# First layer's tanh of images 1 to 7 as Exp, Ln, Exp in chunks, with the limit on VectorE right behind the sum

## Chip, cores and metric

One core of a Trainium2 chip runs the whole program. The metric is the device time of one execution in microseconds; the median of three runs is given, and one further execution was profiled.

## The reference

Eight images of 128 channels and 36 x 36 pixels go through two layers. The change lies in the first:

```python
# layer 0, per image; xn is the group-normed image through a 1x1 convolution
q = conv3x3(xn, w_qx)                     # 36 x 36 queries
k, v = conv3x3(xn, w_kx, 'VALID'), conv3x3(xn, w_vx, 'VALID')   # 34 x 34
a_x = v @ softmax(q @ k)                  # attention over the 1156 keys
h = tanh(conv1x1([xn, a_x, context], w_h) + b_h)
x = x + conv1x1(h, w_o) + b_o
# layer 1, per image: additive attention of 1296 tokens,
#   scores = w . tanh(q_i + k_j), softmax, weighted sum; then a gated mixture of experts
```

The context term is the same for every pixel, so with b_h it is one column, `hb`. The output of layer 0 of an image is the input of its layer 1.

## The kernel before

**The main loop.** The scores of layer 1 take nearly all the time. They are written as sums of quotients of exponentials: for each image (8), chunk of 432 queries (3) and tile of 128 keys (11, the last of 16 keys), twelve *slots* (two for the last tile) each compute a denominator and a numerator by matmuls. There are 2,928 slots. In one slot, `denominators` lets TensorE make `d` in PSUM (two buffers) and ScalarE (ACT) take its Ln (L999); at the end of a group of one or two slots ACT takes Exp of minus that (L1002), the reciprocal. `numerators` lets TensorE make `n` in PSUM (four banks, shared with all other matmul results outside the scores). `terms` lets VectorE (DVE) multiply `n` by the reciprocal, either into `rp` (L1033, three buffers) that GpSimd (POOL) adds up (L1040, L1042), or in place (L1027), added up on DVE (L1029). Denominators are issued three slots ahead. At the end of a tile POOL folds the sums (L1049, L1051) and ACT takes their Exp (L1062).

**Background work.** While image b is in its main loop, image b+1 is prepared in a lane of generators: `normal`, `conv_keys`, `layer0`, `tokens`, `keys`. Each engine runs its instructions in the order in which they were issued, so the place of a background instruction in the slots sets what stands behind it. A generator says at each yield whether it goes on to matmuls (`matmuls(rest)`) or not (`step(rest)`, `TAKE` is a step without rest), and how many slots it rests first. `take_turns` runs due steps at the start of a slot (not in the four slots of twelve whose products DVE adds up itself), `matmul_turn` runs due matmuls in every third slot, after that slot's terms, as far as a pace in matmul columns allows; several turns can follow one another there.

**The first layer.** `layer0(b)` computes v, then per chunk of 432 pixels (`NCH` = 3): the queries by `conv_turns`, four turns of three matmuls `pc`, each followed at `TAKE` by copies or sums on DVE (L312 to L316); the scores `s`, their Exp on ACT (L471), the sums on POOL (L462); the weighted values `pa`, their scaling by a reciprocal made of Ln and Exp (L485, L486, L499, L500); and the convolution of x, `px`, that is added into the chunk's columns of `hp` (L506). The tile `hp` is named hpre in the profile. After the three chunks one ACT instruction takes tanh of all 1,296 columns with the bias `hb` (L509). The tanh isn't in the set of tables that has Ln and Exp, so a table load stands ahead of it (counted to L509), and `preload_act_table_set(LNEXP)` loads the other set again (L510). Then the three matmuls `po` (w_o) follow, and DVE adds them to the image (L517).

Image 0 is prepared before the main loop, with no slots around it. Images 1 to 7 are prepared in the background of images 0 to 6.

Of the kernel before, what the change touches and what calls it, by code (L numbers as in the profile page):

```python
# [11 lines left out]
AF = mybir.ActivationFunctionType  # L12
ALU = mybir.AluOpType
AX = mybir.AxisListType

NB, C, H, W = 8, 128, 36, 36
# [6 lines left out]
RC = H // NCH  # L23
# [49 lines left out]
def kernel(  # L73
# [28 lines left out]
    nc = tc.nc  # L102
# [27 lines left out]
    with ExitStack() as loop, ExitStack() as score:  # L130
# [22 lines left out]
        def big_tile(name):  # L153
            return big.tile([128, NT * 128], F32, tag="big", name=name)

        def chunk_tile(name):
            return chunks.tile([128, CH], F32, tag="chunk", name=name)

        def aux(name):
            return ps_n.tile([128, 512], F32, tag="n", name=name)  # L160
# [40 lines left out]
        ones = const.tile([128, 128], F32, tag="ones", name="ones")  # L201
# [32 lines left out]
        hb = const.tile([C, 1], F32, tag="hb", name="hb")  # L234
# [20 lines left out]
        LNEXP = "natural_log_exp_and_others"  # L255
# [16 lines left out]
        TAKE = (False, 0)  # L272

        def step(rest=1):
            return (False, rest)

        def matmuls(rest=0):
            return (True, rest)
# [3 lines left out]
        def bmm(out, lhsT, rhs, **kw):  # L282
            behind[0] += max(out.free_size(), 128) + 20
            mm(out, lhsT, rhs, **kw)  # L284
# [9 lines left out]
        def conv_turns(taps, rows, y0, dst, inner):  # L294

            r0, nr = rows
            even, odd = ((1, slice(1, WV, 2)), (0, slice(0, WV, 2))) if inner else (
                (0, slice(0, W, 2)), (0, slice(1, W, 2)))
            for j in range(4):
                ps = aux("pc")[:, : nr * HW]  # L300
                for dy in range(3):
                    bmm(ps, taps[:, dy, j, :],
                        xwin[:, j, (y0 + dy + r0) * HW : (y0 + dy + r0 + nr) * HW],
                        start=(dy == 0), stop=(dy == 2))
                yield TAKE
                ps = ps.rearrange("p (a b) -> p a b", b=HW)
                for (t0, cols), used in ((even, j < 3), (odd, j > 0)):
                    if used:
                        d = dst[:, :, cols]
                        m = ps[:, :, t0 : t0 + d.shape[-1]]  # L310
                        if j == 0 or (j == 1 and cols is odd[1]):
                            nc.vector.tensor_copy(d, m)  # L312
                        elif j == 2 and cols is odd[1]:
                            nc.vector.tensor_sub(d, d, m)
                        else:
                            nc.vector.tensor_add(d, m, d)  # L316
                yield matmuls()
# [13 lines left out]
        def load_taps(name):  # L331
            if name in raw_taps:
                return raw_taps.pop(name)[0]
            t = big_tile(name)[:, : 12 * C]
            nc.sync.dma_start(t, turned_taps[name])
            return t.rearrange("p (y j c) -> p y j c", y=3, j=4)
# [68 lines left out]
        def grid(t, width):  # L405
            return t.rearrange("p (a b) -> p a b", b=width)

        def conv_keys(b):
# [3 lines left out]
            for r0, nr in KROWS:  # L412
                yield from conv_turns(
                    taps["k"], (r0, nr), 1, grid(k[:, r0 * WV : (r0 + nr) * WV], WV), True
                )

        def layer0(b):

            r = xs[b][:, :N]
            k = convolved.pop("k")  # L420
            while gates:
                yield step()
            wv_t = load_taps("wv_t")
            v = big_tile("v0")
            wq_t = load_taps("wq_t")
            yield matmuls(3)
            for r0, nr in KROWS:
                yield from conv_turns(
                    wv_t, (r0, nr), 1, grid(v[:, r0 * WV : (r0 + nr) * WV], WV), True
                )  # L430
            yield matmuls(1)

            vw = big_tile("vw")[:DT, : NDT * C].rearrange("p (j c) -> p j c", c=C)
            for g in range(0, NDT, 4):
                some = DTILES[g : g + 4]
                tp = aux("pvw")
                for j, (o, n) in enumerate(some):
                    bmm(tp[:n, j * C : (j + 1) * C], v[:, o : o + n], wh_s[:, 1, :],
                       start=True, stop=True)
                yield TAKE  # L440
                full = sum(n == DT for _, n in some)
                nc.vector.tensor_copy(
                    vw[:, g : g + full, :],
                    tp[:DT, : full * C].rearrange("p (j c) -> p j c", c=C),
                )
                for j in range(full, len(some)):
                    n = some[j][1]
                    nc.vector.tensor_copy(vw[:n, g + j, :], tp[:n, j * C : (j + 1) * C])
                yield matmuls()
            hp = big_tile("hpre")[:, :N]  # L450
            for c in range(NCH):
                cols = slice(c * CH, (c + 1) * CH)
                q = chunk_tile("q0")
                yield from conv_turns(wq_t, (c * RC, RC), 0, grid(q, W), False)
                yield matmuls(1)
                tot = chunk_tile("tot0")
                ex = []

                def total(j):
                    n = DTILES[j][1]  # L460
                    of = ex[0] if j == 1 else tot
                    nc.gpsimd.tensor_add(tot[:n], of[:n], ex[j][:n])  # L462

                ax = chunk_tile("ax0")
                for j0 in range(0, NDT + 2, 2):
                    for o, n in DTILES[j0 : j0 + 2]:
                        ps = aux("s0")
                        bmm(ps[:n, :CH], k[:, o : o + n], q, start=True, stop=True)
                        yield TAKE
                        e = chunk_tile("e0")  # L470
                        nc.scalar.activation(e[:n], ps[:n, :CH], AF.Exp)  # L471
                        ex.append(e)
                        if len(ex) > 2:
                            total(len(ex) - 2)
                        yield matmuls()
                    if j0 == 0:
                        continue
                    if j0 == NDT:
                        total(NDT - 1)
                        yield matmuls(3)  # L480
                        ri = chunk_tile("ri0")
                        pt = aux("pt0")
                        bmm(pt[:, :CH], ones[:DT], tot[:DT], start=True, stop=True)
                        yield TAKE
                        nc.scalar.activation(ri, pt[:, :CH], AF.Ln)  # L485
                        nc.scalar.activation(ri, ri, AF.Exp, scale=-1.0)  # L486
                        yield matmuls()

                    pa = aux("pa0")[:, :CH]
                    for j in (j0 - 2, j0 - 1):  # L490
                        n = DTILES[j][1]
                        bmm(pa, vw[:n, j, :], ex[j][:n], start=(j == j0 - 2), stop=(j == j0 - 1))
                    yield TAKE
                    if j0 == 2:
                        nc.vector.tensor_copy(ax, pa)
                    elif j0 < NDT:
                        nc.vector.tensor_add(ax, pa, ax)
                    else:
                        nc.vector.tensor_add(pa, pa, ax)  # L499
                        nc.vector.tensor_mul(ax, pa, ri)  # L500
                    yield matmuls()
                px = aux("px1")
                bmm(px[:, :CH].rearrange("p (a b) -> p a b", b=W), wh_s[:, 0, :],
                   xpad[:, 1 + c * RC : 1 + (c + 1) * RC, 1 : 1 + W], start=True, stop=True)
                yield TAKE
                nc.vector.tensor_add(hp[:, cols], px[:, :CH], ax)  # L506
                yield matmuls()
            yield step(2)
            nc.scalar.activation(hp, hp, AF.Tanh, bias=hb)  # L509
            nc.scalar.preload_act_table_set(LNEXP)  # L510
            yield matmuls(2)
            for c in range(NCH):
                cols = slice(c * CH, (c + 1) * CH)
                po = aux("po0")
                bmm(po[:, :CH], wo_s, hp[:, cols], start=True, stop=True)
                yield TAKE
                nc.vector.scalar_tensor_tensor(  # L517
                    r[:, cols], po[:, :CH], bo_s, r[:, cols], ALU.add, ALU.add
                )
                yield matmuls()  # L520
# [629 lines left out]
        for p, (u, k) in enumerate(slots):  # L1150
            b, c, j = units[u]
# [181 lines left out]
    for h in range(NB // 2):  # L1333
        for c in range(NCH):
            cols = slice(c * CH, (c + 1) * CH)
# [76 lines left out]
```

## Time and profile before

| | |
|---|---|
| median of 3 runs | 6119.27 us (6111.72 to 6121.77) |
| the profiled execution | 6131.19 us |
| its span | 6129.5 us |
| mean granted TensorE clock | 0.982 |
| busy: PE, DVE, ACT, POOL | 92%, 78%, 87%, 75% |
| main loop, ACT alone: Ln L999, Exp L1002 | 2483.2 and 2495.8 us |
| tanh L509 | 8 x 1.376 us |
| table loads at L509 and L510 | 8 x 1.283 us each |

PE is TensorE's matmuls. Line numbers are of the kernel before. A row of a group gives the instructions of a line with output and inputs, shapes and count, their busy time and the mean duration in ns, and then the idle time of the engine ahead of them with what ended it. A row of a timeline gives start and duration in us, engine, line, operation and count, and in brackets the idle time of the engine ahead of it and who ended it; a matmul in fp32 stands there as two records. In a row of windows, the engines' busy times are in the order PE, weight loads, DVE, ACT, POOL; after them come the granted clock of TensorE as a share of full speed (PEclk), the busy share of the DMA engines and their GB/s.

### The profile page before, as it was taken

Reading aid. Unit: us, or ns where it says so; the run is one execution under the profiler, and the core shown is the slowest. Engines: PE = TensorE matmul, PEld = TensorE weight load, DVE = VectorE, ACT = ScalarE, POOL = GpSimd, SP = SyncE. Lnnn points to the kernel's source line nnn. Section 1 sums busy time; section 2 is a strip of 40 time slices with the busy share of each in tenths; the row PEclk is TensorE's granted clock in tenths of the full one; section 3 lists DMA queues with packets and bytes.
Section 4 is the critical chain, followed back from the end, with each engine's and each line's share of the span. In section 5 each row is a group of like instructions: output and inputs, shape, how many; then the busy total and the mean of one; then the engine's idle time right before and its main releaser. Section 6 shows DMA issues by size and latency. Waiting matters only on the chain.

```text
span 6129.5 us, 94280 instructions
## 1 busy us (share of the span) xinstructions
PE 5669.4 (92%) x33500; PEld 2928.9 (48%) x33500; DVE 4786.5 (78%) x9544; ACT 5338.2 (87%) x5859; POOL 4603.0 (75%) x2824
## 2 busy tenths in 40 slices
PE   7999999999999999999999999999999999988886
PEld 5554455544554445544445444454445544544433
DVE  4787878878788788877787777887778878788883
ACT  1999898998989989889998999899998998999991
POOL 4777777877778867778687786877777777777871
PEclk9999999999999999999999999999999999999998
DMA  1210021001110011100111001110011000110008
GB/s 44 73 34 22 25 74 40 20 25 33 66 39 20 26 46 54 37 24 23 61 39 39 22 24 65 40 33 23 28 62 49 24 25 28 66 50 29 28 20 286
DMA packets 150409, 270.42 MB, mean 44 GB/s; under 512 B 45553, under 2 KB 75633, under 8 KB 149937
## 3 DMA queue, kind: packets, MB, share of 16 engines
q1 hardware_dynamic: 149936, 264.39, 13.0%
q8 instruction: 264, 4.33, 0.3%
q14 instruction: 209, 1.70, 0.1%
HBM read 200.15 MB, written 63.93 MB: 43 GB/s over the span
## 4 chain that ended last, share of the span: by engine, by line
PE 54%; DVE 16%; ACT 15%; issue 11%; POOL 2%; DMA 1%; SPq 0%; DVEq 0%; POOLq 0%; ACTq 0%
PE d L976 18%; PE n L976 12%; ACT lq L999 11%; PE pa L284 7%; DVE rp L1033 7%; PE pc L284 5%; DVE n L1027 5%; PE s L284 3%; DVE accd L1029 2%; PE pq L284 2%; PE pk L284 1%; PE d L981 1%; PE n L981 1%; ACT e L1062 1%; DMA w<-in_weight_dram 1%
## 5 line engine op out<-in xcount | busy, mean ns | idle before, releaser
L1042 POOL TENSOR_TENSOR accp<-accp,rp 128x864 f32<-128x864 f32 x1439 | 2912.2, 2024 | 995.3 <-DVE rp L1033 951.4
L976 PE MATMUL d<-qf,kf 32*128 32x432 f32 (+1 forms) x11520 | 2785.5, 562 | 269.3 <-ACT lq L999 264.0
L976 PE MATMUL n<-qf,kf 32*128 32x432 f32 (+1 forms) x11520 | 2997.9, 556 | 31.0 <-DVE rp L1033 12.4
L999 ACT ACTIVATE lq<-d 128x864 f32<-128x864 f32 x2928 | 2483.2, 877 | 473.9 <-PE n L976 284.6
L1033 DVE TENSOR_TENSOR rp<-n,lq 128x432 f32<-128x432 f32 x3912 | 2180.2, 600 | 757.5 <-PE n L976 606.3
L1002 ACT ACTIVATE lq<-lq 128x864 f32<-128x864 f32 (+1 forms) x1944 | 2495.8, 1284 | 61.7
L976 PEld LDWEIGHTS d<-qf,kf 32*128 32x128 f32 (+1 forms) x11520 | 1024.4, 185 | 1447.4 <-ACT lq L999 1105.5
L976 PEld LDWEIGHTS n<-qf,kf 32*128 32x128 f32 (+1 forms) x11520 | 1263.1, 186 | 700.4 <-issue 294.8
L1029 DVE TENSOR_TENSOR accd<-n,accd 128x432 f32<-128x432 f32 x1440 | 866.1, 601 | 24.6
L1027 DVE TENSOR_TENSOR n<-n,lq 128x432 f32<-128x432 f32 x1440 | 810.3, 607 | 59.1 <-PE n L976 37.1
L1040 POOL TENSOR_TENSOR accp<-rp 128x864 f32<-128x864 f32 x240 | 485.6, 2023 | 286.6 <-DVE rp L1033 284.4
L284 PE MATMUL pa<-xh,e 128*108 128x129 f32 x1920 | 254.9, 281 | 32.7 <-DVE accd L1029 27.7
L284 PEld LDWEIGHTS pa<-xh,e 128*108 128x108 f32 x1920 | 221.0, 174 | 127.4 <-DVE accd L1029 102.6
L1051 POOL TENSOR_TENSOR accd<-accp,accd 128x432 f32<-128x432 f32 x239 | 265.4, 1110 | 18.7
L1049 POOL TENSOR_TENSOR accp<-accp 128x432 f32<-128x432 f32 x239 | 263.9, 1104 | 11.8
L711 POOL TENSOR_SCALAR qf<-qf,cs_s 128x432 f32<-128x432 f32 x192 | 260.3, 1366 | 9.2 <-ACT qf L710 9.2
L462 POOL TENSOR_TENSOR tot<-tot,e 116x432 f32<-116x432 f32 x192 | 212.2, 1105 | 9.0 <-ACT e L471 4.5
L284 PE MATMUL s<-q,k 128*116 128x432 f32 x480 | 207.0, 547 | 7.8 <-DVE accd L1029 5.5
L471 ACT ACTIVATE e<-s 116x432 f32<-116x432 f32 x240 | 116.3, 521 | 99.1 <-PE s L284 97.9
L284 PE MATMUL pa<-e,vw 116*128 116x432 f32 x480 | 196.8, 532 | 0.4
L284 PEld LDWEIGHTS pk<-xT,a_k 128*128 128x128 f32 x1408 | 164.8, 192 | 54.2 <-DVE accd L1029 43.5
L1022 DVE TENSOR_TENSOR accd<-n,lq 128x432 f32<-128x432 f32 x240 | 143.8, 599 | 49.6 <-ACT lq L1002 26.3
(223 smaller groups left out, 3826.5 us busy)
## 6 DMA issues: line engine op xcount, KB each, us to landing
kf<-kd SPq DMA_DIRECT2D x239, 512.0 KB
kd<-ks SPq DMA_DIRECT2D x158, 256.0 KB
w<-in_weight_dram SPq DMA_DIRECT2D x32, 1024.0 KB
wk_t<-wk_t_d SPq DMA_DIRECT2D x7, 768.0 KB
wv_t<-wv_t_d SPq DMA_DIRECT2D x7, 768.0 KB
wq_t<-wq_t_d SPq DMA_DIRECT2D x7, 768.0 KB
x<-in_x_dram SPq DMA_DIRECT2D x8, 648.0 KB
t<-tokd SPq DMA_DIRECT2D x96, 54.0 KB
```

The lines of the kernel that those rows point to most:

```text
L284: mm(out, lhsT, rhs, **kw)
L711: nc.gpsimd.tensor_scalar(qf[:, 1, :], qf[:, 0, :], cs_s[:, q : q + 1], None, ALU.mult)
L976: mm(outs[h][:, :CH], kf[rows[h], q, :], qf_of[b, c, q][rows[h], part, :], start=True, stop=True)
L999: nc.scalar.activation(lq[:, o : o + n, :], d[:, :n, :CH], AF.Ln)
L1002: nc.scalar.activation(some, some, AF.Exp, scale=-1.0)
L1027: mult(ns[h], ns[h], lq[:, o + h, :])
L1029: nc.vector.tensor_add(live["d"], ns[h], live["d"])
L1033: mult(rp[:, h, :], n, lq[:, o + h, :])
L1040: nc.gpsimd.tensor_add(live["p"], live["r"], rp)
L1042: ending(u if k == NP - 1 else 0).tensor_add(live["p"], live["p"], rp)
L1049: ending(u).tensor_add(s[:, 0, :], s[:, 0, :], s[:, 1, :])
L1051: ending(u).tensor_add(d, s[:, 0, :], d)
```

## The change

For images 1 to 7, tanh is written as tanh(y) = 1 - 2 exp(-ln(1 + exp(2y))). Each chunk's columns are treated on their own. Right behind the sum of L506, DVE adds `hb` and limits the values to 15 at most (`limited`). Three more functions are put into a queue, `late`: `exp` and `log` on ACT, and `share`, which is another Exp on ACT and a multiplication and addition on POOL. Chunks 0 and 1 have theirs taken one at a time at the `TAKE`s of the next chunk's query convolution, ahead of that turn's DVE copies. Those of chunk 2 are taken one at a time after a `step(1)` each. Exp and Ln are in the set of tables that the scores use. Image 0 keeps its tanh with the two loads, and the `step(2)` ahead of it is gone.

```diff
+        def tanh_parts(h):
+
+            def limited():
+                nc.vector.tensor_scalar(h, h, hb, 15.0, ALU.add, ALU.min)
+
+            def exp():
+                nc.scalar.activation(h, h, AF.Exp, scale=2.0)
+
+            def log():
+                nc.scalar.activation(h, h, AF.Ln, bias=ones[:, 0:1])
+
+            def share():
+                nc.scalar.activation(h, h, AF.Exp, scale=-1.0)
+                nc.gpsimd.tensor_scalar(h, h, -2.0, 1.0, ALU.mult, ALU.add)
+
+            return limited, exp, log, share
+
         def layer0(b):
...
             hp = big_tile("hpre")[:, :N]
+            late = deque()
             for c in range(NCH):
                 cols = slice(c * CH, (c + 1) * CH)
                 q = chunk_tile("q0")
-                yield from conv_turns(wq_t, (c * RC, RC), 0, grid(q, W), False)
+                for says in conv_turns(wq_t, (c * RC, RC), 0, grid(q, W), False):
+                    yield says
+                    if late and says == TAKE:
+                        late.popleft()()
                 yield matmuls(1)
+                assert not late
                 tot = chunk_tile("tot0")
...
                 yield TAKE
                 nc.vector.tensor_add(hp[:, cols], px[:, :CH], ax)
+                if b > 0:
+                    limited, *parts = tanh_parts(hp[:, cols])
+                    limited()
+                    late.extend(parts)
                 yield matmuls()
-            yield step(2)
-            nc.scalar.activation(hp, hp, AF.Tanh, bias=hb)
-            nc.scalar.preload_act_table_set(LNEXP)
+            if b == 0:
+                nc.scalar.activation(hp, hp, AF.Tanh, bias=hb)
+                nc.scalar.preload_act_table_set(LNEXP)
+            while late:
+                yield step(1)
+                late.popleft()()
             yield matmuls(2)
```

## The prediction

> **What bounds the kernel now.** I read the page first, then the ScalarE groups by line, then the timelines of all engines around one tanh (image 6's background work makes image 7's first layer, at 5146 us), then the table of windows.
>
> ```profile
> span 6129.5 us, 94280 instructions
> PE 5669.4 (92%) x33500; PEld 2928.9 (48%) x33500; DVE 4786.5 (78%) x9544; ACT 5338.2 (87%) x5859; POOL 4603.0 (75%) x2824
> ...
> L509 ACT ACTIVATE hpre<-hpre,hb 128x1296 f32<-128x1296 f32 x8 | 11.0, 1376 | 1.2 <-DVE hpre L506 1.1
> ...
> L509 ACT ACT_TABLE_LOAD x8 | 10.3, 1283 | 0.1
> L510 ACT ACT_TABLE_LOAD x8 | 10.3, 1283 | 0.1
> ```
>
> No engine is the bound everywhere: PE is busy 92%, ACT 87%. So the stretch around the change decides. There the tanh and its two table loads keep ACT from the scores for 3.98 us (5146.79 to 5150.77):
>
> ```profile
> 5146.79 1.28 ACT L509 ACT_TABLE_LOAD   x1
> 5148.09 1.38 ACT L509 ACTIVATE hpre<-hpre,hb 128x1296 f32<-128x1296 f32 x1
> 5149.48 1.28 ACT L510 ACT_TABLE_LOAD   x1
> 5150.77 0.89 ACT L999 ACTIVATE lq<-d 128x864 f32<-128x864 f32 x1
> ...
> 5151.72 0.63 PE L976 MATMUL d<-qf,kf 32*128 32x432 f32 x2 [3.88 <-ACT lq L999]
> ...
> 5154.17 1.81 PE L976 MATMUL d<-qf,kf 64*128 64x432 f32 x4 [1.27 <-ACT lq L999]
> ...
> 5157.35 3.37 PE L284 MATMUL po<-hpre,w_o 128*128 128x432 f32 x6
> ...
> 5161.69 0.89 ACT L999 ACTIVATE lq<-d 128x864 f32<-128x864 f32 x1 [3.10 <-PE n L976]
> ```
>
> See three things. PE idles 3.88 us behind the block. Then PE is slow: the four d records take 1.81 where the same row shows 1.00 at 5145.09. And ACT then loses another 3.10 us waiting for that slow PE. The windows agree (us, busy by engine, PEclk):
>
> ```profile
> 5060.00:5120.00 60.00, 57.37 (x332) 29.14 (x329) 47.63 (x96) 55.48 (x64) 53.30 (x34) 1.00 0.07 22
> 5120.00:5180.00 60.00, 52.47 (x276) 25.66 (x276) 48.52 (x106) 53.53 (x56) 38.30 (x23) 0.94 0.11 32
> ```
>
> **What the Trainium skill says.** (1) "ScalarE: Activation LUTs", sections "What ACT_TABLE_LOAD costs" and "Table sets: the hidden batching unit": a load is 1283 ns plus a drain of about 1380 ns, and natural_log_exp_and_others holds both exp and ln. The trace agrees on 1283; a drain does not show (ACT idles 0.1 us over 8 loads). (2) "TensorE: Matmul & The Clock Gate", section "What's actually happening": PE's clock halves after an idle window of about 3.4 us, until it has been busy for one. The trace has PEclk 0.94 over the 60 us with the tanh, a loss of 3.6 us, so about 7 us at half rate. (3) "VectorE: DVE Perf Modes", section "Mode 2×_2P": an fp32 tensor_scalar from SBUF to SBUF uses both read ports. The trace fits: L325, 128x384 with one input, takes 353 ns, L326 of the same size with two takes 608. (4) "SBUF — State Buffer", section "SBUF: two separate sides": such an op shares a port pair with GpSimd under an exclusive lock, and the later one blocks for the whole instruction of the other. The trace agrees, on a tensor_scalar of 11 columns:
>
> ```profile
> L260 DVE TENSOR_SCALAR ve<-ln_mv x8: 173/1693/1701, 142.6 to 5184.7; 128x11 f32<-128x11 f32 x8
> ```
>
> It takes 173 ns once, with POOL free, and about 1693 ns in the others, which run beside a POOL add of 2.02 us and end with it.
>
> **The change part by part,** for one of seven images (1 to 7).
>
> *Removed: the block.* 3.98 us of ACT, and ACT has no idle time in the 7 us before it and only 0.18 in the 8 after: all 3.98 is on the path.
>
> *Removed: the slow clock behind it.* From the d at 5154.17 to the next d at 5160.65 PE is busy 6.48 us at half rate. At full rate elsewhere: d to n 0.83 and n to the next 0.82 (5013.92, 5014.75, 5015.57), and three 432 column matmuls 2.36 (the s of 5032.08, next d 5034.44): 4.01. That is 2.47 less, and ACT's wait of 3.10 shrinks to 0.63. So 2.47 on the path too. Together 6.45.
>
> *Added on ACT: nine pieces.* Exp in SBUF is 563 ns (L486). Ln with a bias column I take as L1062's 640. Neighbours overlap by 0.09 (L1062 starts 5140.39, the next 5140.94), so a chunk's pieces cost 0.47 + 0.55 + 0.47 = 1.49. ACT's busy time rises by 3 x 1.77 - 3.94 = 1.4 us an image. Where they land decides:
> - Chunk 2's run at three successive steps in the stretch above, where ACT has no idle: 1.49 on the path. By the step counts the po matmuls keep their turn.
> - Chunk 1's exp and log are issued with the two conv turns of 5015.57, before an Ln for which ACT idles 1.47 us: free. If that cover is gone, 1.02. Its share comes with the turn of 5021.83, into 19 us without ACT idle: 0.47.
> - Chunk 0's log and share come with the turns of 4942.71, before an Ln for which ACT idles 1.31: free, with the same cost if not. Its exp waits for the limit, next.
>
> *Added on DVE: the limit,* 432 columns, SBUF to SBUF. By L325's 353 for 384 I take 0.38. It is put right behind L506, ahead of the next score products, so it depends on POOL. In chunks 1 and 2 POOL is idle at that time (its adds ended at 5012.37 and 5138.52; the limit would start at 5012.95 and 5139.2). DVE's products are 0.38 late, the PE buffers as much: I take 0.3 and 0.2, bounds 0 and 0.38 each. Chunk 0 is different:
>
> ```profile
> 4938.35 0.60 DVE L506 TENSOR_TENSOR hpre<-px,ax 128x432 f32<-128x432 f32 x1
> 4938.94 0.38 DVE L312 COPY q<-pc 128x216 f32<-128x216 f32 x1
> 4939.99 1.12 DVE L1033 TENSOR_TENSOR rp<-n,lq 128x432 f32<-128x432 f32 x2 [0.66 <-PE n L976]
> ...
> 4938.58 2.03 POOL L1042 TENSOR_TENSOR accp<-accp,rp 128x864 f32<-128x864 f32 x1 [1.19 <-DVE rp L1033]
> ...
> 4939.88 0.89 ACT L999 ACTIVATE lq<-d 128x864 f32<-128x864 f32 x1 [1.10 <-PE n L976]
> ```
>
> The POOL add starts while L506 runs and ends at 4940.61. The limit must wait for it and ends at about 4940.95. Behind it on DVE stand the copy and the products of 4939.99 (then 4941.3, 1.3 late). ACT's exp waits for the limit until 4941.0 and takes to 4941.5, and the Ln of 4939.88 stands behind that: 1.6 late. The next d on PE (4940.82) waits for this Ln, and from there PE was the bound (ACT idles 1.31, 0.90, 1.40, 1.62 for it up to 4956). So 1.6 on the path. Without the lock it would be 0 to 0.4.
>
> *Added on POOL:* three tensor_scalars of about 1.3 us (L324's mean 1268 for 384 columns, L711's 1366 for 432). POOL idles about 1.1 us between its adds there and 6.2 us ahead of the add of 5158.73; chunk 2's comes after the add that ends at 5152.5 and must be done for the last po matmul, about two slots of 2 us later. Each waits for its exp; behind it stand the score adds, and DVE for their rp buffers. ACT runs ahead of POOL by several slots, so I cost it nothing; if po waits, up to 1 us. Image 0 keeps its tanh; its dropped step stands in a part that runs without slots, so it costs nothing. No DMA is added or moved, and SP's queue is not touched.
>
> **Sum:** 6.45 - 1.49 - 0.47 - 0.3 - 0.2 - 1.6 = 2.4 us an image, 17 us for seven. The profiled execution took 6131.2, so a like one would take 6114; from the median 6119.3 it is 6102.6. What is late next: PE in chunk 0's and 1's stretches, ACT in chunk 2's.
>
> **Rivals.**
> - *No lock on the limit* (the lock is seen here on 11 columns, not on 432): chunk 0 costs 0.3 and not 1.6. 3.7 an image: 6093. Against it stand the seven blocked rows.
> - *The clock drops behind chunk 0's limit, and the kernel gets slower.* PE would idle from 4940.56 to 4942.45, 1.9 us of a window of 3.4. Drops already follow waits of 1.1 to 1.4 us near 4690 (PEclk 0.96 there). One of 6.8 us at half rate where PE is the bound costs up to 3.4: 2.4 - 3.4 = -1.0 an image, 6126. It decides where a drop costs more than 2.4 in the mean of the images, so at 3.4 it must come in five of seven.
> - *ACT becomes the bound* and hides no piece: another 1.02 for each of chunks 0 and 1: 0.4 an image, 6117. Against it: ACT's idle rows there name PE.
> - *The loads stay*, if Exp and Ln alternated between sets: six loads of 1.28 an image and more, 5.3 us slower an image, 6156. Against it: one load at the start serves all Ln and Exp of the scores now.
>
> **How the numbers follow.** The forecast has 0.42, no lock 0.17, the clock drop 0.25, ACT the bound 0.11, loads or something unseen on the slow side 0.05. 0.2% is 12.2 us, about what a measurement of this kernel tells from no change. Of the forecast's 0.42, with its bounds of about 1 us an image (6095 to 6111), 0.29 is over 0.2% faster; all of no lock is. The drop, with 0 to 3.4 us an image and drops elsewhere that shift with the phase, gives 0.10 same and 0.15 slower; ACT the bound 0.07 same and 0.04 slower. Sum: 0.46 faster, 0.30 same, 0.24 slower. For 8 in 10 the range goes from 6087 (no lock, bounds in favour) to 6130 (the drop and some waits at po).
>
> **What would show it.** Right: one tanh and two of its loads left; no drop of PEclk behind where the tanhs were; the limit's row x21 with a mean near 0.9 us, some 0.38 and seven near 2.0; the Ln behind chunk 0's exp 1.6 late; images of about 735 us where they take 737 to 741 from tanh to tanh. Wrong: all 21 limits at 0.4 (no lock); half clock right after chunk 0's limit (the drop); PE waiting for ACT at 5016 and 4943 (ACT the bound).

## The result, and the profile after

The changed kernel takes 6111.23 us (median of 22 runs, 6104.40 to 6116.83) against 6118.79 of before (22 runs, 6111.72 to 6131.01). The ratio is 0.9986, with an interval of 0.9980 to 0.9993: about 0.14% faster, 8 us. A second measurement gave 0.9982 (0.9973 to 0.9990), 10.6 us. The forecast was 6102.6 with a range of 6087 to 6130: some 17 us were expected, and 8 to 11 came.

The page after, its span, its engines, and the rows of the lines that took the place of L509 and L510 (from the groups by line: busy us, mean ns, then the idle time ahead and who ended it):

```profile
span 6106.2 us, 94348 instructions
...
PE 5658.5 (93%) x33500; PEld 2920.2 (48%) x33500; DVE 4805.0 (79%) x9565; ACT 5340.4 (87%) x5901; POOL 4615.2 (76%) x2845
```

```profile
L426 ACT ACTIVATE hpre<-hpre,ones 128x432 f32<-128x432 f32 x21 | 13.6, 646 | 0.2
...
L423 ACT ACTIVATE hpre<-hpre 128x432 f32<-128x432 f32 x21 | 11.6, 552 | 14.1 <-DVE hpre L420 14.1
L429 ACT ACTIVATE hpre<-hpre 128x432 f32<-128x432 f32 x21 | 11.6, 552 | 0.2
...
L535 ACT ACTIVATE hpre<-hpre,hb 128x1296 f32<-128x1296 f32 x1 | 1.4, 1375 | 1.1 <-DVE hpre L528 1.1
...
L535 ACT ACT_TABLE_LOAD x1 | 1.3, 1283 | 0.0
L536 ACT ACT_TABLE_LOAD x1 | 1.3, 1283 | 0.0
```

One tanh and its two loads are left, for image 0. ACT is busy 2 us more than before, not less. L423, the first Exp, carries 14.1 us of waits for the limit, L420. That limit and the last step on POOL, seen by tile (min, median and max ns):

```profile
L420 DVE TENSOR_SCALAR hpre<-hpre,hb x21: 445/446/1854, 501.3 to 5121.4; 128x432 f32<-128x432 f32 x21
...
L430 POOL TENSOR_SCALAR hpre<-hpre x21: 549/554/564, 514.4 to 5135.2; 128x432 f32<-128x432 f32 x21
```

446 ns is the limit alone. Seven of the 21, all of chunk 0, stand beside a POOL add and take 1782 to 1854 ns. Here is one, in the timeline of all engines (start, duration in us, and in brackets the idle time ahead):

```profile
4918.39 0.59 DVE L528 TENSOR_TENSOR hpre<-px,ax 128x432 f32<-128x432 f32 x1
4918.61 2.01 POOL L1071 TENSOR_TENSOR accp<-accp,rp 128x864 f32<-128x864 f32 x1 [1.18 <-DVE rp L1062]
...
4919.02 1.85 DVE L420 TENSOR_SCALAR hpre<-hpre,hb 128x432 f32<-128x432 f32 x1
...
4920.79 0.37 DVE L312 COPY q<-pc 128x216 f32<-128x216 f32 x1
4920.90 0.56 ACT L423 ACTIVATE hpre<-hpre 128x432 f32<-128x432 f32 x1 [2.09 <-DVE hpre L420]
4921.08 1.11 DVE L1062 TENSOR_TENSOR rp<-n,lq 128x432 f32<-128x432 f32 x2
...
4921.37 0.87 ACT L1028 ACTIVATE lq<-d 128x864 f32<-128x864 f32 x1
```

The POOL add ends at 4920.62 and the limit at 4920.87. Behind it stand the products (L1062) on DVE, and behind L423 the next Ln of the scores (L1028) on ACT. In the stretch of the tanh the same view shows this now:

```profile
5126.34 0.55 ACT L423 ACTIVATE hpre<-hpre 128x432 f32<-128x432 f32 x1
...
5129.29 0.64 ACT L426 ACTIVATE hpre<-hpre,ones 128x432 f32<-128x432 f32 x1
...
5132.30 0.55 ACT L429 ACTIVATE hpre<-hpre 128x432 f32<-128x432 f32 x1
...
5133.68 0.99 PE L1005 MATMUL d<-qf,kf 64*128 64x432 f32 x4 [1.90 <-ACT lq L1028]
...
5135.33 2.44 PE L284 MATMUL po<-hpre,w_o 128*128 128x432 f32 x6
...
5138.74 0.89 ACT L1028 ACTIVATE lq<-d 128x864 f32<-128x864 f32 x1 [0.93 <-PE n L1005]
```

PE's longest wait there is 1.90 us where it was 3.88. The po matmuls take 2.44 us where they took 3.37, and ACT waits 0.93 for PE where it waited 3.10. The window that answers to the 60 us around the tanh of before:

```profile
5102.60:5162.60 60.00, 55.43 (x296) 27.06 (x296) 53.77 (x118) 55.41 (x61) 42.95 (x27) 1.00 0.12 32
```

PEclk (third from the end) is 1.00, it was 0.94. This holds for the image shown. In two of the seven images of this profile, PE's clock is halved for 3.41 us behind the same wait of 1.90; d and po are then slower (compare their rows in the view before):

```profile
2189.29 1.37 PE L1005 MATMUL d<-qf,kf 64*128 64x432 f32 x4 [1.90 <-ACT lq L1028]
...
2192.03 3.00 PE L284 MATMUL po<-hpre,w_o 128*128 128x432 f32 x6
```

**Place by place.** The slots come in the same order in all these kernels, so the starts of ACT's Ln of the scores can be compared one by one. How much later (+) or earlier (-) than in the first profile of before a stretch of slots ends, relative to its begin, is the table's number: us an image, mean over images 1 to 7. Of an image's 366 slots, chunk 0 is slots 170 to 185, chunk 1 is 195 to 222, *tanh* is 264 to 289, *tokens*, the piece behind the po matmuls, is 290 to 310, and *early* is the first 80. Nothing was edited in *tokens* and *early*.

| kernel | chunk 0 | chunk 1 | tanh | tokens | early |
|---|---|---|---|---|---|
| before again | 0.00 | -0.01 | +0.01 | +0.04 | 0.00 |
| changed | +1.10 | +0.91 | -4.69 | 0.00 | -0.58 |
| changed, again | +1.10 | +0.91 | -4.46 | +0.99 | -0.49 |
| tanh left out | 0.00 | -0.01 | -6.54 | -0.36 | -0.49 |
| idle TensorE kept busy | 0.00 | -0.01 | -2.43 | +0.09 | -1.23 |
| limit alone | +0.96 | +0.48 | -0.56 | -0.27 | -1.30 |
| pieces a turn later | +0.97 | +0.92 | -4.66 | +0.66 | -0.37 |
| limit from PSUM | +0.19 | +1.04 | -4.12 | -1.00 | -1.38 |
| limit from PSUM, pieces paired | +0.19 | +0.78 | -4.14 | -0.55 | -1.15 |
| no limit | +0.01 | +0.39 | -3.82 | -0.23 | -1.20 |

The first profile of before is one of its slowest runs (6131 us, median 6119). The columns of chunks 0 and 1 can be read as they stand, because no half clock stands there in these profiles. *Tokens* and *early*, and in part *tanh*, also hold what TensorE's clock did in the two runs compared. The row of the limit alone shows by how much in *tanh*: that kernel has the tanh and its loads, and still reads -0.56. Single executions of before lie up to 20 us apart on one chip (6116.25 to 6136.75).

### The profile page after: what moved, and what is told of

Same layout as the page of the kernel before. It is cut to its first block, busy times and chain, and to the rows that moved or that the text cites. A ratio compares the mean times of both kernels' runs of the same rounds, so it can differ in the third digit from the quotient of the medians.

```text
span 6106.2 us, 94348 instructions
## 1 busy us (share of the span) xinstructions
PE 5658.5 (93%) x33500; PEld 2920.2 (48%) x33500; DVE 4805.0 (79%) x9565; ACT 5340.4 (87%) x5901; POOL 4615.2 (76%) x2845
## 4 chain that ended last, share of the span: by engine, by line
PE 53%; DVE 17%; ACT 15%; issue 11%; POOL 2%; DMA 1%; SPq 0%; DVEq 0%; POOLq 0%; ACTq 0%
PE d L1005 17%; PE n L1005 12%; ACT lq L1028 11%; PE pa L284 7%; DVE rp L1062 7%; DVE n L1056 5%; PE pc L284 5%; PE s L284 3%; DVE accd L1058 2%; PE pq L284 2%; PE pk L284 1%; PE d L1010 1%; PE n L1010 1%; ACT e L1091 1%; DMA w<-in_weight_dram 1%
## 5 line engine op out<-in xcount | busy, mean ns | idle before, releaser
L1028 ACT ACTIVATE lq<-d 128x864 f32<-128x864 f32 x2928 | 2482.5, 877 | 434.6 <-PE n L1005 260.4
L1062 DVE TENSOR_TENSOR rp<-n,lq 128x432 f32<-128x432 f32 x3912 | 2180.1, 600 | 747.2 <-PE n L1005 601.8
L284 PE MATMUL pk<-xT,a_k 128*128 128x128 f32 (+1 forms) x1408 | 180.6, 281 | 0.2
```

What stands on the lines that cost most here:

```text
L1028: nc.scalar.activation(lq[:, o : o + n, :], d[:, :n, :CH], AF.Ln)
L1062: mult(rp[:, h, :], n, lq[:, o + h, :])
```

## The experiments

**Before again.** The same program, another execution.

> The kernel before, profiled in another execution. Theory A (the block costs the same in every run): TensorE at half clock for 6.8 us behind all seven tanhs of images 1 to 7 as in the first profile, and 737 to 741 us from one tanh to the next. Theory B (the half clock depends on where TensorE's idle 3.9 us fall in the windows of 3.41 us in which the clock is set, so the profile of before, at 6131 us the slowest of its runs, showed more of it than usual): behind some of the tanhs no half clock or 3.4 us of it, the stretch from there 1 to 2.5 us shorter in those images, and a time of 6112 to 6122 us.

6126.94 us. TensorE at half clock stands behind all seven tanhs again, 6.8 us each:

```profile
5150.15 0.63 PE L976 MATMUL d<-qf,kf 32*128 32x432 f32 x2 [3.88 <-ACT lq L999]
...
5152.60 1.81 PE L976 MATMUL d<-qf,kf 64*128 64x432 f32 x4 [1.43 <-ACT lq L999]
...
5155.78 3.45 PE L284 MATMUL po<-hpre,w_o 128*128 128x432 f32 x6
```

The same 3.88 us of waiting stands there, d (1.81) runs at half rate, and so does a part of po (3.45). From tanh to tanh it takes 737.1 to 740.8 us. Theory A holds for this run. But it is a slow one too (median of before on this chip 6120.76), so alone it doesn't rule out theory B. Two runs further down speak against B. With TensorE kept busy, the medians lie 18 us apart. And with the limit alone, the profiled execution (6126.36) lies near its median (6125.86), and half clock of 6.8 us or more stands at all seven tanhs. There, though, PE's wait is 3.42 us and the half clock begins before its end in six of them, and the place is 0.56 us shorter in the mean, so where the half clock falls may matter. An execution of before at its own median was not profiled.

**Idle TensorE kept busy.** To the kernel before:

```diff
             nc.scalar.preload_act_table_set(LNEXP)
+            if b > 0:
+                yield step(1)
+                warm = aux("warm")
+                for _ in range(5):
+                    mm(warm[:, :CH], wo_s, r[:, :CH], start=True, stop=True)
             yield matmuls(2)
```

> The kernel before with five matmuls of 432 columns put into TensorE's idle 3.9 us behind each tanh, their results unused. ACT's block of 3.98 us stays. Theory A: the half clock behind the tanh goes, 2.47 us in each of seven images, 17 us: 6102 us, like the changed kernel. Theory B: the half clock is there only in a part of the executions, so 5 to 10 us are won: about 6110 us. Rival C (the extra matmuls stand ahead of the scores' and delay them): 0.5 us an image is lost where no half clock was, and the time is 6117 to 6122 us.

6102.69 us, ratio 0.9968 (0.9955 to 0.9980): 18 us faster, with the tanh, its loads and ACT's block untouched. The stretch of the tanh ends 2.43 us earlier in the mean (2.15 to 2.65 in single images), close to the 2.47 that the prediction worked out for the slow clock. PE is busy where it idled, and the po matmuls are back at full rate (timeline of this kernel):

```profile
5124.52 3.89 PE L515 MATMUL warm<-x,w_o 128*128 128x432 f32 x10
...
5133.60 2.44 PE L284 MATMUL po<-hpre,w_o 128*128 128x432 f32 x6
```

Theory A. Five matmuls whose results nobody reads gain 18 us, more than the 8 to 11 of the change.

**Without the tanh.** The tanh of images 1 to 7, its bias and its loads are left out of the kernel before.

> The kernel before without the tanh of images 1 to 7 and without its two table loads (that part of the computation is left out; the bias goes with it). It shows what removing the block is worth before anything is paid for. Theory A: 3.98 us of ACT and 2.47 us of slow TensorE an image, 45 us: 6074 us. Theory B: 3.98 us an image in full and the clock only at times: 28 to 38 us: 6081 to 6091 us. Rival D (TensorE or DVE would take over as the bound there): under 20 us, over 6099 us.

6078.57 us, ratio 0.9931 (0.9918 to 0.9944): 42 us. The stretch ends 6.54 us earlier, where 6.45 had been forecast. Rival D falls. The time alone doesn't tell A from B, since its interval is 34 to 50 us; the place speaks for A.

**The limit alone.** To the kernel before:

```diff
                 nc.vector.tensor_add(hp[:, cols], px[:, :CH], ax)
+                if b > 0:
+                    nc.vector.tensor_scalar(hp[:, cols], hp[:, cols], hb, 15.0, ALU.add, ALU.min)
...
-            nc.scalar.activation(hp, hp, AF.Tanh, bias=hb)
+            if b == 0:
+                nc.scalar.activation(hp, hp, AF.Tanh, bias=hb)
+            else:
+                nc.scalar.activation(hp, hp, AF.Tanh)
```

> The kernel before with the limit on VectorE behind each chunk's sum for images 1 to 7, at the same place as in the changed kernel; the tanh and its loads stay, only its bias is now added by the limit. Theory A (VectorE's own delay by the lock is on the path): chunk 0's limit takes 1.85 us beside the GpSimd add and costs 1.2 us an image, chunks 1 and 2 up to 0.4 each: 8 to 14 us slower, 6127 to 6133 us. Rival E (only ScalarE's Exp that waits for the limit makes it costly): under 0.4 us an image, within 3 us of before.

6125.86 us, ratio 1.0009 (1.0001 to 1.0017), 5 us slower: less than forecast, but the places are clear. Chunk 0 costs 0.96 us and chunk 1 0.48. The limit is the one of the changed kernel:

```profile
L508 DVE TENSOR_SCALAR hpre<-hpre,hb x21: 444/446/1852, 501.7 to 5134.9; 128x432 f32<-128x432 f32 x21
```

No Exp waits for the limit here, and chunk 0 still pays 0.96 of the changed kernel's 1.10. So the delay of DVE is enough by itself; rival E falls. What the limit costs in chunk 2 can't be read from the table, as its -0.56 shows.

**Pieces a turn later.** To the changed kernel:

```diff
-                    if late and says == TAKE:
+                    if late and says == TAKE and (i > 0 or c > 1):
                         late.popleft()()
```

with i counting the yields of `conv_turns`. The pieces of chunk 0 are taken while c is 1, and they come one turn later. Those of chunk 1 are taken while c is 2, and the condition leaves them where they were, contrary to what the expectation says.

> The changed kernel with the pieces of chunks 0 and 1 taken one turn of the convolution later, so that chunk 0's Exp no longer waits for the blocked limit ahead of the scores' Ln. If the prediction's path over ScalarE (1.6 us) was the one that counted, 1.2 us an image go and it takes 6103 us. If VectorE's delay alone is enough, as the run with the limit alone says (1.04 us of the 1.2), 0.2 us an image at most goes in chunk 0, chunk 1 pays up to 0.5 for a piece that comes among busy ScalarE slots: 6109 to 6115 us.

6110.45 us, ratio 0.9975 (0.9965 to 0.9985), on a chip whose before had 6125.63. Chunk 0 is at 0.97, as with the limit alone (0.96), so ACT's wait for the limit added 0.13 us to what the delay of DVE costs. Chunk 1 is at 0.92 because its pieces didn't move: in the trace they stand at the same slots as in the changed kernel. So the expectation for chunk 1 was not tried. By the places, nearly nothing is won.

**The limit from PSUM.** To the changed kernel:

```diff
-                nc.vector.tensor_add(hp[:, cols], px[:, :CH], ax)
-                if b > 0:
-                    limited, *parts = tanh_parts(hp[:, cols])
-                    limited()
+                if b == 0:
+                    nc.vector.tensor_add(hp[:, cols], px[:, :CH], ax)
+                else:
+                    nc.vector.tensor_add(px[:, :CH], px[:, :CH], ax)
+                    _, *parts = tanh_parts(hp[:, cols])
+                    nc.vector.tensor_scalar(hp[:, cols], px[:, :CH], hb, 15.0, ALU.add, ALU.min)
                     late.extend(parts)
```

> The changed kernel, but the sum of each chunk stays in PSUM and the limit reads it there and writes the chunk's columns in SBUF[...]. Theory A (chunk 0's cost is the lock): all 21 limits take about 0.66 us, none near 1.85, the 1.2 us of chunk 0 go; chunk 1 pays up to 0.2 more for the longer limit. 0.9 to 1.2 us an image, 6 to 8 us under the changed kernel's 6111: about 6104 us. Rival F (any instruction behind the sum delays the products as much): nothing won, 6111 us or more.

6103.52 us, ratio 0.9963 (0.9950 to 0.9977). All 21 limits take the same time now:

```profile
L533 DVE TENSOR_SCALAR hpre<-px,hb x21: 667/668/669, 502.1 to 5106.3; 128x432 f32<-128x432 f32 x21
```

Seven of them, those of chunk 0, lie wholly inside a POOL add of 2.02 us and take no longer than the others. The sum ahead of the limit stays in PSUM in this kernel as well. A limit that takes half as long again when alone (668 ns against 446) is never blocked, and chunk 0 falls from 1.10 to 0.19. Chunk 1 pays 0.13 more. Theory A: chunk 0 paid for the wait behind the POOL add, and not for one more instruction ahead of the products.

**The limit from PSUM, pieces paired.** In addition, log and share of chunks 0 and 1 in one turn:

```diff
                     if late and says == TAKE:
                         late.popleft()()
+                        if len(late) == 1:
+                            late.popleft()()
```

> The limit from PSUM, and the log and share of chunks 0 and 1 both taken at the second turn of the convolution, where ScalarE waits 1.3 to 1.5 us for TensorE. Theory A: chunk 1's share leaves the stretch in which ScalarE has no idle time, 0.47 us an image less than with the limit from PSUM alone: about 6101 us. Rival H (the waits of 1.3 and 1.5 us do not hold log and share together with the rest): no difference to the limit from PSUM, or 0.5 us an image more.

6096.74 us, ratio 0.9950 (0.9937 to 0.9963), the lowest median of the kernels that compute the tanh in full with its limit, and faster than both the kernel before and the changed one. Chunk 1 falls from 1.04 to 0.78, about half of the forecast 0.47. By its interval the time is not told from that of the limit from PSUM alone.

**No limit.** The changed kernel without its limit, the bias in the first Exp (scale 2, bias twice hb).

> The changed kernel without the limit of 15 (that step is left out; the bias goes into the first Exp as a column of twice its value). Theory A: chunk 0 loses its 1.2 us, chunk 1 the 0.48 of the limit, the Exp's bias costs 0.1 each in chunk 2: 1.5 us an image, 10 us under the changed kernel: about 6101 us. Rival G (the difference to the forecast lies in TensorE's clock at other places and not in the limit): under 5 us, 6106 us or more.

6098.04 us, ratio 0.9954 (0.9942 to 0.9966). Chunk 0 costs 0.01, chunk 1 0.39, which is the price of its share alone. Theory A on these two, and more is won than rival G allows. Whether the difference to the forecast lies in TensorE's clock, this run doesn't decide. Its *tanh* column (-3.82) is low because half clock follows chunk 2's pieces in five of its seven images. By its interval it is no different from the limit from PSUM with paired pieces.

**The changed kernel again.**

> The changed kernel again, beside before on the same chip. If the difference to the forecast is TensorE's clock at other places: ScalarE's start times differ from before by +1.2 us (chunk 0), +0.9 (chunk 1) and -4.7 (the stretch of the tanh) an image as in the first profile, while the stretches of half clock stand elsewhere than in that profile, and the mean granted clock is 0.986 to 0.987 against 0.983 to 0.984 of before: 6 to 14 us faster. If the first profile was the exception: other sums at the three places, or a difference of 17 us or more.

6111.31 us against 6121.91, ratio 0.9982 (0.9973 to 0.9990). The three places give +1.10, +0.91 and -4.46, as before within 0.23. The other columns moved: *tokens* is +0.99 here and 0.00 in the first profile of the same program. The mean granted clock is 0.9860 here (0.9862 in the first 22 runs), against 0.9836 for before on the same chip (0.9831 and 0.9835 on two others).

## Why the prediction was half right

- **The block and the slow clock behind it, 6.45 us an image: right.** 6.54 measured with the tanh left out, and of this 2.43 by the clock (2.47 forecast), measured by keeping TensorE busy. One reading was loose: of the 6.48 us from d to d only those up to 5159.25 ran at half clock (PEclk is 0.61 over the whole). The price doesn't suffer, as it compares measured lengths.
- **Chunk 2's pieces, 1.49 on the path, and the limit's 0.2: near in the mean, by luck in part.** 6.45 - 1.69 = 4.76; measured 4.69 and 4.46. But single images save 4.8 to 5.3 us, or else 3.3 to 3.7 in two or three of seven. The second kind, in both profiles, are those with 3.4 us of half clock about 12 us behind chunk 2's limit. That drop was not in the sum. It stands right behind PE's wait of 1.90 us for the Ln behind share. The wait is the same in all 14 images of the two profiles, and half clock follows in five of them; why in these was not settled. So a gain above the forecast and a drop that it left out nearly cancelled.
- **Chunk 0: right in kind, a little high, and the wrong path named.** The lock came in all seven images, 1.78 to 1.85 us (about 2.0 forecast). The cost is 1.10, forecast 1.6. The prediction had DVE's products 1.3 late and ACT's Ln 1.6 late, and priced the Ln. The limit alone (0.96) and chunk 0's pieces a turn later (0.97) show that the delayed products on DVE carry nearly all of it.
- **Chunk 1: 0.77 forecast, 0.91 measured.** The limit is 0.48 and not 0.3; it had been bounded at 0.38, and takes 446 ns. The share is 0.39 to 0.43 (0.47).
- **POOL's steps: nothing, as forecast.** They take 554 ns and not 1.3 us, and the last one ends at 5135.70, ahead of the last po matmul.
- **The sum: the clock term did not last.** The places give -4.69 + 1.10 + 0.91 = -2.7 us an image, and -2.45 in the second profile: 17 to 19 us, the forecast's 2.4 and 17. Only 8 to 11 arrived. The term that was mis-sized is "2.47 on the path too", taken seven times: right at its place, and not kept in the whole.
- **Where the rest went.** The mean clock says it. Time lost to the clock is (1 - clock) x time. On the chip where both were run side by side it is 100 us for before (0.9836) and 86 for the changed kernel (0.9860), 15 less. Seven stretches of 6.8 us at half rate should have taken 24 away. So some 9 us of lost clock came back in other places. The profiles show some of it: behind chunk 2, and in *tokens*, where four of seven images pay 2.2 to 2.4 us more in the second profile. For the kernel with TensorE kept busy the loss fell from 101 to 68, by more than 24, and there the whole gain arrived. The single executions of that chip (17 of before, 13 of the changed kernel) agree. In straight lines fitted to them, 0.001 of clock goes with 3.3 and 3.9 us of time. At an equal clock of 0.985 the lines give 6116.3 and 6114.5. So by this estimate some 2 us of the 10.4 between the means, give or take 2, aren't clock, and the clock gave 8 to 9 us where the forecast had 2.47 x 7 = 17. This rests on sums and on how time and clock go together; no run forces the half clock, and what moves it to other places stays open.
- **Rivals.** No lock: wrong. The clock drop behind chunk 0's limit: it did not come; neither profile of the changed kernel has half clock at any of the seven places. A drop came behind chunk 2 instead. ACT as the bound: wrong for chunk 0, whose pieces cost 0.13 beside the limit; in chunk 1 they cost no more than the share. The loads stay: wrong, two are left.

## What to carry to other kernels

A short VectorE op can take four times its own length by what POOL is doing when it is issued: here the limit, with input and output in SBUF, waited out a running POOL add, and with its input in PSUM it did not. Price the end of a stall as well as the stall: here over a third of what the tanh cost (2.43 of 6.54 us) was TensorE running at half clock afterwards, and five useless matmuls in the gap got that back without touching the tanh. When a gain is made of clock, price what the change may do to the clock elsewhere, and compare the mean clock of many runs, because a profile shows the drops of one execution.

## What the hardware showed

- A fp32 tensor_scalar of 128x432, SBUF to SBUF on DVE, takes 446 ns alone and up to 1854 beside a POOL add of 2.02 us; from PSUM it takes 667 to 669 ns in all 21, seven of them beside such an add.
- On POOL a tensor_scalar with two constants takes 554 ns for 128x432, where L711 with a column of factors takes 1366.
- A wait of PE of 1.90 us, not only one of 3.88, was followed by half clock, in five of 14 images; behind the wait of 3.88 it came in all 14 of the two profiles of before.
- Two executions of the same changed program differ by 12.5 us (6107.87 and 6120.37) with the same times at every edited place to 0.25 us.
